# A four-layer sequence kernel: edge tokens in the first query block, more places for background pieces, and the last FFN of two blocks beside the attention

## The chip, the cores and the metric

The kernel runs on one core of one Trainium2 chip. The metric is the device time of one execution in microseconds (us). A NeuronCore has five engines with a queue of instructions each: TensorE (PE; its weight loads are shown apart as PEld), VectorE (DVE), ScalarE (ACT), GpSimd (POOL) and SyncE (SP), which here only issues DMA transfers. An engine works off its own queue in order and waits on semaphores for the others.

## The reference

The input is x of 2048 tokens by 128 features. Four layers follow each other, each adds an attention-like part and a feed-forward part (FFN) to x behind a layer norm (`ln`):

```python
x = x + L0_attn(ln(x))   # 16 heads of width 8
x = x + L0_ffn(ln(x))    # 128 -> 512 -> 128, exact GELU
x = x + L1_attn(ln(x))   # 16 heads of width 64 over all 2048 tokens
x = x + L1_ffn(ln(x))    # silu(x Wg) * (x Wu), 384 hidden, 8-bit weights
x = x + L2_attn(ln(x))   # each token attends to itself and its two neighbours, cyclic in 1024
x = x + L2_ffn(ln(x))    # best one of 8 experts, a 128x128 matrix each
x = x + L3_attn(ln(x))   # a memory: 32 chunks of 64 tokens, one gradient step per chunk
x = x + L3_ffn(ln(x))    # best two of 8 experts and a shared one, 176 hidden each
```

What matters for the order of the work: L1's attention needs all keys and values, but its queries can be taken block by block. Everything behind it works token by token, except for two things. L2's attention needs the first neighbours beyond a block of tokens on either side. L3's memory is serial: step c starts from the state that step c-1 left.

```python
g = grad_fn(W_state, k[:, sl], v[:, sl]) * 0.1        # sl: the chunk's 64 tokens
gn = maximum(norm(g), 1e-6); g = g * minimum(1.0 / gn, 1.0)
(S_state, W_state), Wtraj = scan(step, (S_state, W_state), (g, eta, theta, alpha))
```

## The kernel before

All engine calls are made in one function, `body` (line 71), through a wrapper (`Eng`, line 137), so every row of the profile carries line 147 and the tiles' names tell what it is. The order of the instructions on PE, DVE, ACT and POOL is that of the calls: a planner, run while the program is built, keeps a clock for each engine from cost constants (`note`, line 96) and calls the pieces of many generators in the order that its clocks suggest. The framework places the DMAs on SP.

There are three stretches. The first is layer 0 and the keys and values of layer 1 (0 to 906 us). The second is the **attention stage** (`l1_attn`, line 1066): L1's attention runs over 40 **units**, each one block of queries by one pair of heads. The blocks are the table `QB` in line 33, (first token, tokens, columns): 512, 384, 512, 384 and 256 tokens, with eight pairs each. A unit has 16 **key steps** of 128 keys. A key step is four passes of scores (high part, low parts, and minus the row's maximum) for two heads on PE into two banks, two exponentials P on ACT, then two products with the values on PE. The sums of P over the key steps are taken by POOL (`acg`), and in key steps 14 and 15 by DVE (`acd`). Beside these the maxima of the scores of a later unit are formed (`u_max`, line 425): products km by qh on PE, and a reduction `mx` on DVE that frees the bank. `stage_wo` (line 1023) adds the pairs' share of the output product.

The last stretch is the **tail**: what is left of the layers behind.

Those layers are generators that run in the background of the attention stage: `stage_a` (L1's FFN of 256 tokens), `stage_a2` and `stage_b` (L2's attention), `stage_b2` (its experts), `stage_c` (L3's inputs of 128 tokens), `chunk` (line 1626, one memory step, 32 in all: tiles af, u, ef, dz, rr, gq), `stage_d` (its output), `stage_g` (the router of the last FFN), `stage_e0`, `s_lane` (lines 1872 and 1880, the last FFN: 13 **groups** of up to 128 hidden units per 256 tokens) and `stage_e1` (output). Each `yield` ends a **piece**. A yield says what the next piece needs: a number of PSUM banks (`yield 1`), a time that it should wait (a float), that it has only PE work without a new bank ("T"), or nothing.

`Part.may` (line 202) tells whether a piece may come now: its inputs are due by the planner's clocks, DVE and ACT aren't too far behind, and of the banks that the background uses in the attention stage (the five of `mx`) two stay free. `fill` (line 246) puts pieces into the order until PE's clock has moved by 0.3 us. It is called twice in a key step, behind the maxima and behind the value products (line 1163 on). `fill(lim, "t")` takes only pieces that need neither banks nor PE.

The layers behind need tokens that lie beyond their block: the first tokens of blocks of 256. The **edge tokens** `ex` (1280, 1792 and 2047; line 32) are therefore carried as extra columns by query block 1 (384 tokens, 388 columns), and `stage_m` (line 1314) takes them through L1's FFN to L2's keys and values, into `edge`. `stage_b` of any block waits for `stage_m` ("m" in `s_b`, line 1959), and for `stage_a2` of its neighbour, unless the neighbour's first token is an edge token. `stage_m` can start once query block 1 is through, that is behind unit 15.

In the tail (`tail`, set behind `l1_attn()`) `st`'s three banks join the background's, and five more `s_lane` generators the first two. In the last FFN all groups of a block add into one bank `ac`, which `stage_e0` opens and `stage_e1` adds to x (`xs`) by `add_tok`. In the attention stage `s_e0` lets block b start only when all groups of block b-1 are through.

Of the kernel before, what the change touches and what calls it, by code (L numbers as in the profile page):

```python
# [30 lines left out]
ATANH = (1.0000000039388743, 0.3333315796754013, 0.20012426861749952, 0.13980709417165652, 0.14087328632693624)  # L31
T = dict(lead0=22, more0=4, mgap=0.4, pvq=2, lim0=0.5, fq=(3,), pl=-0.5, pr=1.0, tlow=2, tback=3, late=0.3, pvp="mx", mxp="mx", ex=(1280, 1792, 2047), low=1, lows='ge', keep=1, leave=2, pvn=1, sp=0, rdy=40., eu=2, qg=(22, 16, 10), em=2, el=6, sem=0.2, same=1.2, tsame=3.0, order="hdmBbAaEcCeg", ps=dict(st=3, mx=5), dma=2.3, slack=0.1, lim=0.3, backlog=2.5, lead=(10, 8, 6), pp=7, dve=(14, 15), qp=(1, 1), lanes=2, xl=5,
         QB=[(0, 512, 512), (512, 384, 388), (896, 512, 512), (1408, 384, 384), (1792, 256, 256)])

# [36 lines left out]
def body(ctx: ExitStack, tc: tile.TileContext, x, pa, pb, pc, pi, pd, pr, pr0, pe, pw, out):  # L71
# [122 lines left out]
    class Part:  # L194
# [24 lines left out]
        def step(self):  # L219
            piece[0] = clk["T"]  # L220
            r = next(self.gen, "end")
            self.same = r == "same"
            self.ready = 0.0 if self.same else piece[0] + (r if type(r) is float else 0.0)
            self.pe = r == "T"
            self.banks = r if type(r) is int else 0
            self.seen = len(emitted) if r is False else -1
            if r == "end":
                emitted.add(self.key)
            return r != "end"
# [139 lines left out]
    xnd = dram.tile([128, S], F32, name="xnd")  # L369

    QB = T["QB"]
    EXTRA = T['ex']
    units = [(qb, p) for qb in range(len(QB)) for p in range(NP1)]
    qhh, qfs, kmx, mx1 = {}, {}, {}, {}

    qx = [mid.tile([128, 8], F32R, name=f"qx{i}") for i in range(2)]
    xq = {}

    def u_loadx(qb):
        t0, tn, n = QB[qb]  # L380
        xq[qb] = l1x.tile([128, 512], F32, name="xq", tag="xq", bufs=2)
        if n != tn:
            ge.memset(xq[qb][:, tn:n], 0.0)
            for i, t in enumerate(EXTRA):
                sy.dma_start(xq[qb][:, tn + i:tn + i + 1], xnd[:, t:t + 1])
        sy.dma_start(xq[qb][:, :tn], xnd[:, t0:t0 + tn])

    def u_qprep(u):
        qb, p = units[u]
        if qb not in xq:  # L390
            u_loadx(qb)
        n = QB[qb][2]
        yield 1
        ps = mi()
        mm(ps[:, :n], C("wq", p * 128, 128), xq[qb][:, :n])
        yield
        qf = l1x.tile([128, 512], F32, name="qf", tag="qf")
        se.activation(qf[:, :n], ps[:, :n], AF.Identity, bias=bq8[:, p:p + 1], scale=0.125)
        rel(ps)
        yield  # L400
        qhh[u] = l1q.tile([128, 512], F32R, name="qh", tag="qh")
        se.copy(qhh[u][:, :n], qf[:, :n])
        yield
        qfs[u] = qf
        tn, n = QB[qb][1:]
        if n > tn:
            for e in range(2):
                r = slice(64 * e, 64 * e + 64)
                se.copy(qx[u % 2][r, 4 * e:4 * e + n - tn], qf[r, tn:n])

# [14 lines left out]
    def u_max(u, i):  # L425
# [8 lines left out]
        if 128 * qt == tn:  # L434
            ps = amx()
            mm(ps[0:8], qx[u % 2], kmx[(u, c)])
            ve.tensor_reduce(mx1[u][0:8, 0, 3, c:c + 1], ps[0:8], AX.X, ALU.max)
            rel(ps)
            return 1
# [9 lines left out]
    def u_maxend(u):  # L449
# [6 lines left out]
        if n > tn:  # L456
            ve.tensor_reduce(m[0:8, 0, 3:4], mx[0:8, 0, 3, :], AX.X, ALU.max)
        yield 1
        t = mi()
        if n > tn:  # L460
            te.transpose(t[0:1, 256:264], m[0:8, 0, 3:4], ident[0:8, 0:8])
        for e in range(2):
# [4 lines left out]
        if n > tn:  # L467
            for e in range(2):
                se.mul(mbt[u % 2][64 * e:64 * e + 1, tn:n], t[0:1, 256 + 4 * e:256 + 4 * e + n - tn], -1.0)
        rel(t)  # L470
# [480 lines left out]
    psum_pools(**T["ps"])  # L951
    in0[0] = False
    leave[0] = T["leave"]
# [69 lines left out]
    def stage_wo(qb, part):  # L1023
# [4 lines left out]
        for p in range(2 * part, 2 * part + 2):  # L1028
            mm(ps[:, :n], C("wo", p * 128, 128), O.pop(p)[:, :n], start=(p % 2 == 0), stop=(p % 2 == 1))
            yield  # L1030
        if part == 0:
            w = l1w.tile([128, 512], F32, name="wac", tag="wac", bufs=1)
            se.activation(w[:, :n], ps[:, :n], AF.Identity, bias=bo1)
            rel(ps)
            wacc[qb] = w
            return
# [3 lines left out]
        if part < NP1 // 2 - 1:  # L1040
            return
        del wacc[qb]
        yield 1
        c0, nt = t0 // 128, tn // 128
# [8 lines left out]
        if n != tn:  # L1053
            ne = len(EXTRA)
            xm = edge_x[0] = sm.tile([ne, 128], F32, name="xm", tag="xm", bufs=1)
            for i, t in enumerate(EXTRA):
                sy.dma_start(xm[i:i + 1, :], xs[t % 128:t % 128 + 1, t // 128, :])
            yield 1
# [7 lines left out]
    def l1_attn():  # L1066
        LEAD = dict(zip((256, 384, 512), T["lead"]))
        LEAD.update({260: LEAD[384], 388: LEAD[512]})
        U = len(units)
# [66 lines left out]
        for g in range(16 * U):  # L1136
# [6 lines left out]
            if u + 2 < U:  # L1143
                if k == 1 and units[u + 2][1] == 0:
                    need(("q", u + 1))
                    u_loadx(units[u + 2][0])
                if k == T["qp"][n <= 256] and u + 2 >= EU:
# [13 lines left out]
            for i, (a, b) in enumerate(ops):  # L1161
                for e in range(2):
                    rows = slice(64 * e, 64 * e + 64)
                    mm(pss[e][:, :n], a[rows], b[rows, :n], start=(i == 0), stop=(i == 3), par=e and 0.02)
            for e in range(2):
                pt = pp.tile([128, 512], F32, name="P", tag="P")
# [147 lines left out]
    def stage_m():  # L1314
# [21 lines left out]

        xt = sm.tile([128, 4], F32, name="xtm", tag="xtm", bufs=2)
        yield from norm_T(xt)
        h = sm.tile([128, 12], F32, name="hm", tag="hm", bufs=1)
        for k in range(3):  # L1340
# [3 lines left out]
            yield  # L1344
            th = sm.tile([128, 4], F32, name="thm", tag="thm", bufs=2)
# [3 lines left out]
            ve.scalar_tensor_tensor(h[:, 4 * k:4 * k + ne], th[:, :ne], 0.5, ps[:, 64:64 + ne], ALU.mult, ALU.mult)  # L1349
            rel(ps)  # L1350
            yield 1
        ps = mi()
        for k in range(3):
            mm(ps[:ne, :128], h[:, 4 * k:4 * k + ne], tok(wi, 6 + k), start=(k == 0), stop=(k == 2))
        yield
        ve.tensor_tensor(xm, xm, ps[:ne, :128], ALU.add)
        rel(ps)
        yield
        xt = sm.tile([128, 4], F32, name="xtm", tag="xtm", bufs=2)
        yield from norm_T(xt)  # L1360
        ps = mi()
        for i in range(2):
            mm(ps[:, 4 * i:4 * i + ne], tok(w2m, i), xt[:, :ne])
        yield
        for i in range(2):
            for j, t in enumerate(EXTRA):
                se.activation(edge[:, t // BN, i, int(t % BN > 0):int(t % BN > 0) + 1], ps[:, 4 * i + j:4 * i + j + 1],
                              AF.Identity, bias=b2m[:, i:i + 1])
# [257 lines left out]
    def chunk(b, c):  # L1626
# [48 lines left out]
        ve.scalar_tensor_tensor(u, tht, 2.0, u, ALU.mult, ALU.add)  # L1675
        yield
        mm(da, ef, w2)
# [194 lines left out]
    def stage_e0(b):  # L1872
        d = E[b]
        yield 1
        ac = mi()
        for i in range(BT):
            mm(tok(ac, i), tok(d["rT"][:, 0], i), pes[0:9, 128:256], start=(i == 0), stop=False)
        d["ac"] = ac

    def s_lane(lane):  # L1880

        q = []
        while ("l", NB_ - 1) not in emitted:
# [37 lines left out]
            if d["left"] == 0:  # L1921
                emitted.add(("l", b))
            yield

    def stage_e1(b):
        c0, ac = BT * b, E.pop(b)["ac"]
        add_tok(ac, c0)
        yield
        ov = out.rearrange("(c p) d -> p c d", p=128)
# [188 lines left out]
```

## Time and profile before

| | |
|---|---|
| three timed runs | 2992.95, 3005.0, 3006.38 us (median 3005.0) |
| the profiled execution | 3001.08 us, span 2999.2 us |
| mean granted clock of PE | 0.936 |
| first stretch | 0 to 906 us |
| attention stage | 906 to 2596 us, 1690 us: PE busy 1609.63, DVE 1187.42, ACT 750.20, POOL 1203.47 |
| tail | 2596 to 3000 us, 404 us: PE busy 343.46, DVE 288.45, ACT 159.70, POOL 167.20 |

A row of the profile's groups reads "line engine operation out<-in", the shapes (partitions x elements), the number of instructions, their busy time, the mean of one in ns, and the idle time of the engine just ahead of them with what ended it. A row of the timeline is start, duration, and the same; in brackets stands the wait ahead of it. `mi` is the name of every PSUM bank.

### The profile page before, as it was taken

The numbers are of one execution on the slowest core, as the hardware profiler recorded it, in microseconds if no ns is written. First come the engines' busy times: TensorE is split into PE (matmuls) and PEld (weight loads), VectorE is DVE, ScalarE is ACT, GpSimd is POOL, SyncE is SP. The second block draws the span as 40 slices with busy tenths as digits, with TensorE's granted clock in tenths as the row PEclk, the third lists the DMA queues.
The fourth block names the chain that finished last, engine by engine and source line by source line (L and its number), as shares of the span: only waits on it lengthen the run. The fifth ranks groups of instructions, "written<-read, shape, count | busy, mean of one in ns | idle before, by whom it ended". The sixth has DMA issues, their size and how long they took to land.

```text
span 2999.2 us, 49776 instructions
## 1 busy us (share of the span) xinstructions
PE 2769.9 (92%) x16719; PEld 1307.0 (44%) x16719; DVE 2194.9 (73%) x4699; ACT 1582.9 (53%) x3933; POOL 1522.3 (51%) x1762
## 2 busy tenths in 40 slices
PE   7999999999979899999999999899989898888998
PEld 2222222322234344454444444455544555565666
DVE  7899898898534666566666778887677769787765
ACT  1788887888854444444444444444434334333444
POOL 2400110201127688866776876677767556443444
PEclk9999999999979999999999999999999999776779
DMA  6311231321144333433442332233334343312244
GB/s 142 72 28 22 72 84 17 101 54 46 53 141 135 92 112 110 121 110 111 138 119 87 94 95 87 89 105 108 109 97 114 108 117 94 88 52 61 76 104 115
DMA packets 247749, 275.80 MB, mean 92 GB/s; under 512 B 95747, under 2 KB 183330, under 8 KB 247366
## 3 DMA queue, kind: packets, MB, share of 16 engines
q1 hardware_dynamic: 246630, 272.43, 33.2%
q8 instruction: 132, 2.16, 0.3%
q14 instruction: 123, 1.01, 0.1%
q10 hardware_dynamic: 864, 0.20, 0.0%
HBM read 229.97 MB, written 42.28 MB: 91 GB/s over the span
## 4 chain that ended last, share of the span: by engine, by line
PE 70%; DVE 18%; ACT 6%; issue 3%; DMA 3%; POOL 1%; SPq 0%; ACTq 0%; DVEq 0%; POOLq 0%
PE mi L147 70%; DVE mx L147 5%; ACT P L147 3%; DVE sB L147 1%; DVE o L147 1%; DVE gq L147 1%; DMA ka<-kvd 1%; DVE gt L147 1%; DVE xs L147 1%; ACT kf L147 1%; ACT kh L147 1%; DVE xn L147 1%; DVE sG L147 1%; DVE acd L147 1%; DVE sA L147 0%
## 5 line engine op out<-in xcount | busy, mean ns | idle before, releaser
L147 DVE TENSOR_REDUCE mx<-mi 128x1 f32<-128x512 f32 (+1 forms) x2080 | 1322.1, 683 | 582.8 <-PE mi L147 571.5
L147 ACT ACTIVATE P<-mi 128x512 f32<-128x512 f32 (+3 forms) x2304 | 1137.0, 551 | 1004.1 <-PE mi L147 973.2
L147 POOL TENSOR_TENSOR acg<-acg,P 128x512 f32<-128x512 f32 (+3 forms) x960 | 1011.4, 1083 | 181.8 <-ACT P L147 180.0
L147 PE MATMUL mi<-P,ka 128*64 128x512 f32 (+3 forms) x2560 | 597.6, 546 | 2.3 <-DVE mx L147 2.3
L147 PE MATMUL mi<-qh,ka 64*128 64x512 f32 (+3 forms) x2560 | 521.0, 406 | 9.7 <-DMA ka<-kvd 6.8
L147 PEld LDWEIGHTS mi<-qh,ka 64*128 64x128 f32 x2560 | 247.0, 189 | 382.5 <-issue 347.0
L147 PE MATMUL mi<-kop,qop 48*128 48x512 bf16 x1024 | 348.6, 405 | 24.5 <-DVE mx L147 12.1
L147 PE MATMUL mi<-qop,kop 50*128 50x512 bf16 x1024 | 317.8, 391 | 27.1 <-ACT P L147 24.7
L147 PE MATMUL mi<-P,vop 128*32 128x512 f32 x2048 | 304.3, 623 | 13.9 <-ACT P L147 13.9
L147 POOL TENSOR_SCALAR vep<-mv 128x2 f32<-128x2 f32 (+1 forms) x24 | 5.5, 229 | 495.6 <-DVE mv L147 495.6
L147 PE MATMUL mi<-km,qh 64*128 64x512 f32 x1024 | 225.6, 410 | 30.4 <-DVE mx L147 23.8
L147 PE MATMUL mi<-mbt,onr 64*128 64x512 f32 (+3 forms) x1280 | 228.7, 351 | 1.5 <-DMA mbt<-mb 1.5
L147 PE MATMUL mi<-ql,ka 64*128 64x512 f32 (+3 forms) x1280 | 229.2, 353 | 0.0
L147 PEld LDWEIGHTS mi<-P,ka 128*64 128x64 f32 x2560 | 129.2, 137 | 225.3 <-issue 195.1
L147 PEld LDWEIGHTS <-kop 50*128 50x128 bf16 x1024 | 63.6, 95 | 304.9 <-issue 281.6
L147 POOL TENSOR_TENSOR acg<-P 128x512 f32<-128x512 f32 (+3 forms) x80 | 91.1, 1158 | 202.5 <-DVE acd L147 162.0
L147 PEld LDWEIGHTS mi<-km,qh 64*128 64x128 f32 x1024 | 107.1, 189 | 60.5 <-DVE mx L147 38.5
L147 PEld LDWEIGHTS mi<-mbt,onr 64*128 64x128 f32 x1280 | 124.6, 190 | 13.9 <-DMA mbt<-mb 2.2
L147 PEld LDWEIGHTS mi<-ql,ka 64*128 64x128 f32 x1280 | 125.7, 192 | 0.0
L147 PEld LDWEIGHTS <-qop 48*128 48x128 bf16 x1024 | 72.9, 96 | 97.2 <-issue 82.7
L147 PEld LDWEIGHTS mi<-P,vop 128*32 128x32 f32 x2048 | 55.5, 109 | 119.8 <-issue 90.7
L147 POOL TENSOR_TENSOR kl<-kf,kh 128x512 f32<-128x512 f32 x32 | 40.9, 1278 | 110.9 <-ACT kh L147 82.4
(509 smaller groups left out, 3464.4 us busy)
## 6 DMA issues: line engine op xcount, KB each, us to landing
ka<-kvd SPq DMA_DIRECT2D x320, 384.0 KB
km<-khd SPq DMA_DIRECT2D x159, 256.0 KB
khd<-kh SPq DMA_DIRECT2D x32, 256.0 KB
kvd<-kh SPq DMA_DIRECT2D x32, 256.0 KB
kvd<-kl SPq DMA_DIRECT2D x32, 256.0 KB
kvd<-vt SPq DMA_DIRECT2D x16, 512.0 KB
ka<-in_pw_dram SPq DMA_DIRECT2D x37, 192.0 KB
w3s<-in_pw_dram SPq DMA_DIRECT2D x35, 192.0 KB
```

The source lines that it names most:

```text
L147: r = f(*a, **k)
```

## The change

The diff, cut; what is left out carries a wider edge tile (8 for 4 columns) through `u_maxend` and `stage_m`.

```diff
-T = dict(lead0=22, ..., ex=(1280, 1792, 2047), ...,
-         QB=[(0, 512, 512), (512, 384, 388), (896, 512, 512), (1408, 384, 384), (1792, 256, 256)])
+T = dict(fa=2, ti=(0, 1, 2), tf=1, lead0=22, ..., ex=(256, 768, 1280, 1792, 2047), ...,
+         QB=[(0, 384, 392), (384, 512, 512), (896, 512, 512), (1408, 384, 384), (1792, 256, 256)])
...
-            self.pe = r == "T"
+            self.pe = r == "T" or type(r) is float
...
-    units = [(qb, p) for qb in range(len(QB)) for p in range(NP1)]
+    SEG = [(1, 0, 2), (0, 0, 8), (1, 2, 8), (2, 0, 8), (3, 0, 8), (4, 0, 8)]
+    units = [(qb, p) for qb, p0, p1 in SEG for p in range(p0, p1)]
+    NX = 8
...
-            mm(ps[0:8], qx[u % 2], kmx[(u, c)])
-            ve.tensor_reduce(mx1[u][0:8, 0, 3, c:c + 1], ps[0:8], AX.X, ALU.max)
+            mm(ps[0:2 * NX], qx[u % 2], kmx[(u, c)])
+            ve.tensor_reduce(mx1[u][0:2 * NX, 0, 3, c:c + 1], ps[0:2 * NX], AX.X, ALU.max)
...
-    in0[0] = False
+    in0[0] = True
...
-            yield
+            yield "T" if p % 2 == 0 else 0
-            w = l1w.tile([128, 512], F32, name="wac", tag="wac", bufs=1)
+            w = l1w.tile([128, 512], F32, name="wac", tag="wac", bufs=2)
...
+                if T["tf"] and i in T["ti"]:
+                    fill(9.0, "t")
...
             fill()
+            if T["tf"]:
+                fill(9.0, "t")
...
                     do_pv(*prev.pop(0))
+                    if T["tf"]:
+                        fill(9.0, "t")
                 fill()
+                if T["tf"]:
+                    fill(9.0, "t")
...
-        yield
+        yield "T"
         mm(da, ef, w2)
...
+        own = not tail
-            mm(tok(ac, i), tok(d["rT"][:, 0], i), pes[0:9, 128:256], start=(i == 0), stop=False)
-        d["ac"] = ac
+            mm(tok(ac, i), tok(d["rT"][:, 0], i), pes[0:9, 128:256], start=(i == 0), stop=(own and i == BT - 1))
+        if own:
+            yield
+            add_tok(ac, BT * b)
+        d["ac"] = None if own else ac
...
-            yield T["late"]
+            own = ac is None
+            yield 1 if own else T["late"]
+            if own:
+                ac = mi()
             d["left"] -= 1
+            last = own or d["left"] == 0
             for i in range(BT):
-                mm(tok(ac, i), tok(th[:nr], i), w[:nr, 2, :], start=False, stop=(d["left"] == 0 and i == BT - 1))
+                mm(tok(ac, i), tok(th[:nr], i), w[:nr, 2, :], start=(own and i == 0), stop=(last and i == BT - 1))
+            if own:
+                yield
+                add_tok(ac, BT * b)
...
-            if b and not tail:
-                yield from wait(("l", b - 1))
+            while not tail and b >= T["fa"]:
+                yield False
```

It has three parts.

1. **Edges.** The edge tokens become five (256, 768, 1280, 1792, 2047) and ride with query block 0, now 384 tokens in 392 columns; block 1 is 512. The units run as `SEG` lists them: two pairs of block 1 first, then block 0 whole, then the rest of block 1, then the others. `stage_m` can so start behind unit 9, and `stage_b` needs no neighbour block. The queries' input `xq` is loaded per segment, once more in all; block 1's partial output is held meanwhile in a second `wac` buffer.
2. **Pieces between the passes.** `fill(9.0, "t")` is also called behind the first three score passes, behind each `fill()` and behind the value products. The planner charges 0.12 us where PE's tile shape changes (`in0`), and a piece that waits for a time (float) or a memory step's third product ("T") counts as one that needs PE.
3. **The last FFN beside the attention.** A block whose `stage_e0` comes in the attention stage gives each group a bank of its own, and a sum into `xs` (`add_tok`). Blocks 0 and 1 (`fa` = 2) may do so; the others wait for the tail.

More of the change, by code (lines that the diff above doesn't have):

```diff
@@ L31 @@
 ATANH = (1.0000000039388743, 0.3333315796754013, 0.20012426861749952, 0.13980709417165652, 0.14087328632693624)
-T = dict(lead0=22, more0=4, mgap=0.4, pvq=2, lim0=0.5, fq=(3,), pl=-0.5, pr=1.0, tlow=2, tback=3, late=0.3, pvp="mx", mxp="mx", ex=(1280, 1792, 2047), low=1, lows='ge', keep=1, leave=2, pvn=1, sp=0, rdy=40., eu=2, qg=(22, 16, 10), em=2, el=6, sem=0.2, same=1.2, tsame=3.0, order="hdmBbAaEcCeg", ps=dict(st=3, mx=5), dma=2.3, slack=0.1, lim=0.3, backlog=2.5, lead=(10, 8, 6), pp=7, dve=(14, 15), qp=(1, 1), lanes=2, xl=5,
-         QB=[(0, 512, 512), (512, 384, 388), (896, 512, 512), (1408, 384, 384), (1792, 256, 256)])
+T = dict(fa=2, ti=(0, 1, 2), tf=1, lead0=22, more0=4, mgap=0.4, pvq=2, lim0=0.5, fq=(3,), pl=-0.5, pr=1.0, tlow=2, tback=3, late=0.3, pvp="mx", mxp="mx", ex=(256, 768, 1280, 1792, 2047), low=1, lows='ge', keep=1, leave=2, pvn=1, sp=0, rdy=40., eu=2, qg=(22, 16, 10), em=2, el=6, sem=0.2, same=1.2, tsame=3.0, order="hdmBbAaEcCeg", ps=dict(st=3, mx=5), dma=2.3, slack=0.1, lim=0.3, backlog=2.5, lead=(10, 8, 6), pp=7, dve=(14, 15), qp=(1, 1), lanes=2, xl=5,
+         QB=[(0, 384, 392), (384, 512, 512), (896, 512, 512), (1408, 384, 384), (1792, 256, 256)])
 def _pack_layout(items):
@@ L372, in body, with u_loadx @@
     EXTRA = T['ex']
-    units = [(qb, p) for qb in range(len(QB)) for p in range(NP1)]
+    SEG = [(1, 0, 2), (0, 0, 8), (1, 2, 8), (2, 0, 8), (3, 0, 8), (4, 0, 8)]
+    units = [(qb, p) for qb, p0, p1 in SEG for p in range(p0, p1)]
+    seg = [i for i, (_, p0, p1) in enumerate(SEG) for _ in range(p0, p1)]
+    NX = 8
     qhh, qfs, kmx, mx1 = {}, {}, {}, {}
-    qx = [mid.tile([128, 8], F32R, name=f"qx{i}") for i in range(2)]
+    qx = [mid.tile([128, 2 * NX], F32R, name=f"qx{i}") for i in range(2)]
     xq = {}
-    def u_loadx(qb):
-        t0, tn, n = QB[qb]
-        xq[qb] = l1x.tile([128, 512], F32, name="xq", tag="xq", bufs=2)
+    def u_loadx(i):
+        t0, tn, n = QB[SEG[i][0]]
+        xq[i] = l1x.tile([128, 512], F32, name="xq", tag="xq", bufs=2)
         if n != tn:
[L383 to L386, printed above, removed]
+            ge.memset(xq[i][:, tn:n], 0.0)
+            for j, t in enumerate(EXTRA):
+                sy.dma_start(xq[i][:, tn + j:tn + j + 1], xnd[:, t:t + 1])
+        sy.dma_start(xq[i][:, :tn], xnd[:, t0:t0 + tn])
     def u_qprep(u):
         qb, p = units[u]
-        if qb not in xq:
-            u_loadx(qb)
+        if seg[u] not in xq:
+            u_loadx(seg[u])
         n = QB[qb][2]
@@ L394, in u_qprep @@
         ps = mi()
-        mm(ps[:, :n], C("wq", p * 128, 128), xq[qb][:, :n])
+        mm(ps[:, :n], C("wq", p * 128, 128), xq[seg[u]][:, :n])
         yield
@@ L408, in u_qprep @@
                 r = slice(64 * e, 64 * e + 64)
-                se.copy(qx[u % 2][r, 4 * e:4 * e + n - tn], qf[r, tn:n])
+                se.copy(qx[u % 2][r, NX * e:NX * e + n - tn], qf[r, tn:n])
     def u_qlow(u):
@@ L456, in u_maxend @@
         if n > tn:
-            ve.tensor_reduce(m[0:8, 0, 3:4], mx[0:8, 0, 3, :], AX.X, ALU.max)
+            ve.tensor_reduce(m[0:2 * NX, 0, 3:4], mx[0:2 * NX, 0, 3, :], AX.X, ALU.max)
         yield 1
@@ L460, in u_maxend @@
         if n > tn:
-            te.transpose(t[0:1, 256:264], m[0:8, 0, 3:4], ident[0:8, 0:8])
+            te.transpose(t[0:1, 256:256 + 2 * NX], m[0:2 * NX, 0, 3:4], ident[0:2 * NX, 0:2 * NX])
         for e in range(2):
@@ L468, in u_maxend @@
             for e in range(2):
-                se.mul(mbt[u % 2][64 * e:64 * e + 1, tn:n], t[0:1, 256 + 4 * e:256 + 4 * e + n - tn], -1.0)
+                se.mul(mbt[u % 2][64 * e:64 * e + 1, tn:n], t[0:1, 256 + NX * e:256 + NX * e + n - tn], -1.0)
         rel(t)
@@ L1042, in stage_wo @@
         del wacc[qb]
+        if n != tn:
+            ne = len(EXTRA)
+            xm = edge_x[0] = sm.tile([ne, 128], F32, name="xm", tag="xm", bufs=1)
+            for i, t in enumerate(EXTRA):
+                sy.dma_start(xm[i:i + 1, :], xs[t % 128:t % 128 + 1, t // 128, :])
+            piece[0] = clk["D"]
         yield 1
@@ L1053, in stage_wo @@
         if n != tn:
[L1054 to L1057, printed above, removed]
             yield 1
@@ L1067, in l1_attn @@
         LEAD = dict(zip((256, 384, 512), T["lead"]))
-        LEAD.update({260: LEAD[384], 388: LEAD[512]})
+        LEAD[392] = LEAD[512]
         U = len(units)
@@ L1143, in l1_attn @@
             if u + 2 < U:
-                if k == 1 and units[u + 2][1] == 0:
+                if k == 1 and seg[u + 2] > seg[u + 1]:
                     need(("q", u + 1))
-                    u_loadx(units[u + 2][0])
+                    u_loadx(seg[u + 2])
                 if k == T["qp"][n <= 256] and u + 2 >= EU:
@@ L1335, in norm_T @@
             yield 1
-        xt = sm.tile([128, 4], F32, name="xtm", tag="xtm", bufs=2)
+        xt = sm.tile([128, NX], F32, name="xtm", tag="xtm", bufs=2)
         yield from norm_T(xt)
-        h = sm.tile([128, 12], F32, name="hm", tag="hm", bufs=1)
+        h = sm.tile([128, 3 * NX], F32, name="hm", tag="hm", bufs=1)
         for k in range(3):
@@ L1344, in stage_m @@
             yield
-            th = sm.tile([128, 4], F32, name="thm", tag="thm", bufs=2)
+            th = sm.tile([128, NX], F32, name="thm", tag="thm", bufs=2)
             se.activation(th[:, :ne], ps[:, 0:ne], AF.Tanh, scale=0.5)
@@ L1348, in stage_m @@
             ve.scalar_tensor_tensor(th[:, :ne], th[:, :ne], 1.0, ps[:, 0:ne], ALU.add, ALU.mult)
-            ve.scalar_tensor_tensor(h[:, 4 * k:4 * k + ne], th[:, :ne], 0.5, ps[:, 64:64 + ne], ALU.mult, ALU.mult)
+            ve.scalar_tensor_tensor(h[:, NX * k:NX * k + ne], th[:, :ne], 0.5, ps[:, 64:64 + ne], ALU.mult, ALU.mult)
             rel(ps)
@@ L1353, in stage_m @@
         for k in range(3):
-            mm(ps[:ne, :128], h[:, 4 * k:4 * k + ne], tok(wi, 6 + k), start=(k == 0), stop=(k == 2))
+            mm(ps[:ne, :128], h[:, NX * k:NX * k + ne], tok(wi, 6 + k), start=(k == 0), stop=(k == 2))
         yield
@@ L1358, in stage_m @@
         yield
-        xt = sm.tile([128, 4], F32, name="xtm", tag="xtm", bufs=2)
+        xt = sm.tile([128, NX], F32, name="xtm", tag="xtm", bufs=2)
         yield from norm_T(xt)
@@ L1362, in stage_m @@
         for i in range(2):
-            mm(ps[:, 4 * i:4 * i + ne], tok(w2m, i), xt[:, :ne])
+            mm(ps[:, NX * i:NX * i + ne], tok(w2m, i), xt[:, :ne])
         yield
@@ L1366, in stage_m @@
             for j, t in enumerate(EXTRA):
-                se.activation(edge[:, t // BN, i, int(t % BN > 0):int(t % BN > 0) + 1], ps[:, 4 * i + j:4 * i + j + 1],
+                se.activation(edge[:, t // BN, i, int(t % BN > 0):int(t % BN > 0) + 1], ps[:, NX * i + j:NX * i + j + 1],
                               AF.Identity, bias=b2m[:, i:i + 1])
@@ L1916, in s_lane @@
             ve.scalar_tensor_tensor(th[:nr], th[:nr], 1.0, rb_[:nr], ALU.add, ALU.mult)
-            yield T["late"]
+            own = ac is None
+            yield 1 if own else T["late"]
+            if own:
+                ac = mi()
             d["left"] -= 1
+            last = own or d["left"] == 0
             for i in range(BT):
-                mm(tok(ac, i), tok(th[:nr], i), w[:nr, 2, :], start=False, stop=(d["left"] == 0 and i == BT - 1))
-            if d["left"] == 0:
+                mm(tok(ac, i), tok(th[:nr], i), w[:nr, 2, :], start=(own and i == 0), stop=(last and i == BT - 1))
+            if own:
+                yield
+                add_tok(ac, BT * b)
+                d["done"] = d.get("done", 0) + 1
+                last = d["done"] == NHT3
+            else:
+                last = d["left"] == 0
+            if last:
                 emitted.add(("l", b))
@@ L1926, in stage_e1 @@
         c0, ac = BT * b, E.pop(b)["ac"]
-        add_tok(ac, c0)
-        yield
+        if ac is not None:
+            add_tok(ac, c0)
+            yield
         ov = out.rearrange("(c p) d -> p c d", p=128)
```

## The prediction

> **What bounds the kernel now.** I read the page's totals and slices first, then the stretches of the two stages that the change touches, then single units, and last the waits. The profiled execution took 3001.08 us (span 2999.2), between the three timed runs (2992.95, 3005.0, 3006.38); all sums are against it.
>
> ```profile
> PE 2769.9 (92%) x16719; PEld 1307.0 (44%) x16719; DVE 2194.9 (73%) x4699; ACT 1582.9 (53%) x3933; POOL 1522.3 (51%) x1762
> PE   7999999999979899999999999899989898888998
> PEclk9999999999979999999999999999999999776779
> PE 70%; DVE 18%; ACT 6%; issue 3%; DMA 3%; POOL 1%; SPq 0%; ACTq 0%; DVEq 0%; POOLq 0%
> ```
>
> TensorE (PE) is busy everywhere and is 70% of the chain that ended last, VectorE (DVE) 18%. But the clock row drops to 7 in the slices behind 2550 us: that is the tail, where no attention fills the gaps. By stage (columns: us, then busy PE, PEld, DVE, ACT, POOL, clock, DMA share, GB/s) the attention stage, 906 to 2596 us in two parts, and the tail:
>
> ```profile
> 906.00:1541.00 635.00, 619.83 (x3775) 289.77 (x3776) 387.79 (x646) 301.21 (x645) 486.42 (x454) 0.99 0.39 116
> 1541.00:2596.00 1055.00, 989.80 (x6350) 505.94 (x6347) 799.63 (x1690) 448.99 (x1291) 717.05 (x815) 0.95 0.36 101
> 2596.00:3000.00 404.00, 343.46 (x1715) 256.06 (x1713) 288.45 (x1065) 159.70 (x658) 167.20 (x279) 0.76 0.31 79
> ```
>
> In the attention stage PE is 95% busy at a clock near 1, in the tail 85% at 0.76. So a PE instruction is dearer in the tail than in the attention stage. Moving work forward trades a dear place for a cheap one; the question is whether the cheap place can take it.
>
> **What moves.** I compared the order of instructions on each engine. PE issues 14,895 matmuls in both kernels, but 427 go from the tail (910 to 483) into the attention stage (8225 to 8652). By kind: 26 groups of the last FFN (104 to 78 in the tail), 14 steps of the memory recurrence (18 to 4; the first starts in unit 13 and not in 22), 8 of 10 runs of stage d, 6 of 8 of stage c, 2 of 7 of g. So the change does what it says, and "nothing moves" is no case.
>
> **What the moved work costs in the attention stage.** Prices are start to start of an attention matmul behind the piece, at clock 1. The first half of an FFN group, 1.06 us:
>
> ```profile
> 1597.70 1.13 PE L147 MATMUL mi<-xt,wi 128*128 128x256 f32 x4
> 1598.76 0.50 PE L147 MATMUL mi<-qh,ka 64*128 64x512 f32 x2
> ```
>
> Its second half (two products of 128x128) has no row in this stage; two such (pcs,hb) insert 0.74, so a group is 1.8. A memory step is four small pieces, .58 + .45 + .23 + .46 = 1.72 by the same reading; runs of d 2.5, c 2.6, g 1.7. Sum: 26 x 1.8 + 14 x 1.72 + 8 x 2.5 + 6 x 2.6 + 2 x 1.7 = 46.8 + 24.1 + 20 + 15.6 + 3.4 = **110 us**. The blocks have 2056 columns in all, not 2052; the stage's score and value products are about 1300 us, so +2.5.
>
> The edge rows' larger tiles (16 for 8 rows) are one instruction as before. The extra load of 256 KB of xq and 26 weight loads of 192 KB go onto SP's queue ahead of later ka loads; the DMA share is 0.36 to 0.39 there, and all waits for ka are 20.9 us. I take 0, with as much again, 21, as the upper bound. The change of the planner's price for a tile shape and the new places between passes cost no instruction. The 24 sums that each group with its own bank adds (xs<-xs,mi, 0.44 us a row) are DVE's. Each such group also takes a second bank, of the five that the maxima use, for its product and that sum; a late sum holds the bank, behind which queue the maxima and then PE. That is the same stall as below and is priced there.
>
> **New stalls.** What can late DVE work cost PE? Clean units, in which nothing is inserted, take 40.2 (512 columns) and 34.5 us (384) here:
>
> ```profile
> 1041.50:1081.70 40.20, 40.20 (x236) 17.47 (x234) 24.91 (x41) 20.08 (x37) 33.56 (x26) 1.00 0.37 112
> 1507.00:1541.50 34.50, 33.33 (x236) 17.06 (x234) 23.94 (x42) 16.49 (x38) 26.38 (x26) 1.00 0.44 129
> ```
>
> Summing units by such rows plus the price of what is inserted gives 1586 us for the stage; it took 1690. The 103 us between are stalls, and most have this form:
>
> ```profile
> 2178.15 8.00 DVE L147 SCALAR_TENSOR_TENSOR u<-tht,u 64x32 f32<-64x32 f32 x1
> 2176.28 5.78 POOL L147 TENSOR_TENSOR acg<-acg,P 128x384 f32<-128x384 f32 x6
> 2182.27 3.83 POOL L147 TENSOR_TENSOR acg<-acg,P 128x384 f32<-128x384 f32 x4
> 2187.14 1.39 PE L147 MATMUL mi<-km,qh 64*128 64x512 f32 x2 [6.60 <-DVE mx L147]
> ```
>
> A DVE instruction with its inputs in SBUF, 0.22 us in the tail, lasts 8.00 us across ten of GpSimd's (POOL's) sums; behind it in DVE's queue stand the maxima (mx), whose banks PE needs, and PE waits 6.60 us. Seventeen DVE instructions of the stage last more than 1.5 us over their shortest, together 63 us, 38 of them in memory steps and stage c: 2.7 us for each of the 14 steps. That the mean of the same row differs by stage says so too (xcount, busy, mean ns; the stage, then the tail):
>
> ```profile
> L147 DVE SCALAR_TENSOR_TENSOR u<-tht,u 64x32 f32<-64x32 f32 x14 | 16.0, 1140 | 0.0
> L147 DVE TENSOR_TENSOR gq<-i,dO 32x64 f32<-32x64 f32 x7 | 17.0, 2425 | 0.1
> ```
>
> ```profile
> L147 DVE SCALAR_TENSOR_TENSOR u<-tht,u 64x32 f32<-64x32 f32 x18 | 3.9, 219 | 0.0
> L147 DVE TENSOR_TENSOR gq<-i,dO 32x64 f32<-32x64 f32 x9 | 10.8, 1197 | 0.1
> ```
>
> [...]
>
> For the new stalls I have these ends. Below: the new places between passes let DVE pieces enter up to three times more often in a key step, and in the new order a memory step spans 5 to 6 key steps where it spanned 8 to 12; if that removes the stalls of the 14 old steps as well, -38. Above: if each cluster becomes DVE's. With the stage's own DVE rows I summed what the new order gives each unit: unit 13 has 65 us of DVE against 48 of PE, unit 20 69 against 55, unit 28 58 against 47, unit 36 55 against 39. The heaviest unit before is 22, 47.6 against 44.6, and took 50.2. Eight such dense units times 12 us is +95. The nearest row, 2.7 us a step for 14 more, is +38. I take **+20**: denser memory steps with half the stall each leave the 28 steps at the old sum, and the 26 FFN groups with their 24 DVE sums (some 34 us of DVE) add about half of their time.
>
> So the attention stage is 1690 + 110 + 2.5 + 20 = about 1823.
>
> **What the tail saves.** Its PE instructions are worth 298 us at the stage prices; it took 404, factor 1.356. Left are 298 - 110 = 188, times 1.356 = 255. The middle of the tail is the dearest part:
>
> ```profile
> 2700.00:2800.00 100.00, 86.11 (x386) 62.75 (x385) 69.31 (x264) 37.90 (x177) 40.48 (x69) 0.65 0.27 67
> 2951.00:3000.00 49.00, 40.35 (x205) 32.45 (x204) 24.48 (x51) 21.98 (x56) 22.11 (x28) 0.88 0.45 98
> ```
>
> That part, with 18 memory steps one behind the other (16.3 us apart, 2627 to 2920), shrinks most, which speaks for a few us less; I take 250, a gain of **154**. What is late next is the chain of the last block of tokens, which cannot start before the last output product: in before it ran 16 (wo), 28 (a), 17 (a2), 29 (b), 44 (b2) us to 2730; then c some 30, 4 steps x 16.3 = 65, d and g 31, and the last FFN, 49 before with 23 of 27 half groups behind the last e0, now 17 of 24, so 40. At the old durations this is 300; they were stretched by the work that now leaves, so 300 is the upper end. PE's own 188 at the clock of the last row (0.88) plus its idle 15% is 235 to 250, the lower end.
>
> Sum: 3001 + 110 + 2.5 + 20 - 154 = **2979.5**; I say 2978. The median of the runs shown is 4 us above the profiled execution, so nothing is added for it.
>
> **Rivals.**
> 1. *The places between passes carry DVE's work well.* Old stalls go too (-38 for +20): 1690 + 112 - 38 = 1764, and tail 250: about 2920. For it: memory steps of half the length. Against it: the clusters have more DVE than PE by row sums.
> 2. *The gain is used up.* Stalls grow as before, +38, and the last block's chain keeps the tail at 265 to 300: 3001 + 112 + 38 - 139 = 3012 down to 2997 with a tail of 250; about 3000. For it: 2.7 us a step is the only measured figure.
> 3. *Slower: VectorE becomes the bound in the clusters.* DVE instructions with SBUF inputs lie behind POOL's sums, maxima wait behind them, and PE waits for the maxima's banks. It decides from the point where DVE's row sum of a cluster is above PE's, as it is in units 13, 20, 28 and 36: +95 for +20, so about 3053. For it: those sums. Against it: part of those rows' length is the blocking itself, which a piece entered at a better moment doesn't pay, and maxima may run up to 22 ahead.
>
> **Chances.** Forecast (2960 to 2985) 0.40, rival 1 0.10, rival 2 0.20, rival 3 0.30. A measurement of this kernel can tell about 0.5%, 15 us. Faster is then forecast plus rival 1, 0.50; same 0.20; slower 0.30. Range: rival 1 at 2920 to rival 3 at 3053, 2918 to 3053; the likeliest case alone is 2955 to 2990.
>
> **What would show it.** Right: the last attention unit ends near 1823 - 1690 = 130 us later, the tail is near 250; units that hold memory steps last as long as their clean units plus the inserted PE work; waits for mx stay near their old sum (571.5 us of DVE waiting for mi, PE waiting for mx under 60). Rival 1: the stage ends under 2675, and u and gq rows fall towards 0.2 and 1.2 us. Rival 2: the tail's a to b2 chain keeps 134 us. Rival 3: PE below 90% busy in units 13 to 38, with idle time put down to mx, and DVE near full there. Wrong altogether: if the granted clock in the stage falls below 0.95, which no row of it now suggests, or if ka's loads come late behind the weight loads.

## The result and the profile after

The changed kernel took 3120.08 us (median of 4 runs, 3113.43 to 3125.2) against 3004.75 us for the kernel before: a ratio of 1.0391, 95% interval 1.0358 to 1.0425. It is slower by 115 us; 26 us of gain were forecast, and the time lies outside the range. The page's totals, its slices of PE and of PE's clock, and its chain, after:

```profile
PE 2831.0 (91%) x16719; PEld 1327.6 (43%) x16719; DVE 2301.8 (74%) x4732; ACT 1600.1 (51%) x3930; POOL 1516.3 (49%) x1755
PE   7999999999879999898899989899998888989888
PEclk9999999999889999998889998899998899886878
PE 60%; DVE 22%; ACT 6%; DMA 6%; issue 4%; POOL 1%; SPq 1%; ACTq 0%; POOLq 0%; DVEq 0%
```

PE's share of the chain fell from 70% to 60%, DVE's and the DMAs' rose. The row of the clock, which had its 7s but for one in the tail, now has 8s in many slices of the attention stage. The two stretches (us, then busy PE, PEld, DVE, ACT, POOL, clock, DMA share, GB/s), the attention stage and the tail:

```profile
904.00:2887.00 1983.00, 1827.02 (x10909) 926.11 (x10905) 1426.66 (x2943) 827.59 (x2271) 1256.10 (x1385) 0.91 0.33 96
2887.00:3117.00 230.00, 190.09 (x930) 145.97 (x928) 156.29 (x489) 99.15 (x317) 108.36 (x156) 0.84 0.39 102
```

The tail gave back 174 us (404 to 230). The attention stage took 293 us more (1690 to 1983). To see what it paid for, I split each stretch in three (all in us, from the records of the profile). *Idle* is the sum of the gaps of over 0.15 us between PE's records. *Clock* is half of the time for which the profile's record of the granted clock shows 0.5. *Work* is the rest, my estimate of PE's time at full clock: it takes half clock as half speed, and in the changed kernel four value products of 512 columns (`mi<-P,ka`) in a row take 1.01 us at 1.00 and 1.91 us at 0.50.

| stretch | length | idle | at half clock | clock | work |
|---|---|---|---|---|---|
| attention, before | 1688 | 78 | 116 | 58 | 1551 |
| attention, after | 1983 | 152 | 341 | 171 | 1660 |
| tail, before | 405 | 56 | 195 | 98 | 252 |
| tail, after | 230 | 37 | 73 | 36 | 156 |

The moved work is 109 us in the attention stage (forecast: 112.5). The stage lost 74 us more to idle time and 113 us to the clock. That is 187 us, where I had put 20.

**How one wait becomes both.** The timeline of the changed kernel at 1900 us (start, duration, engine, operation; in brackets the wait ahead), queries for DVE, POOL and PE:

```profile
1900.94 6.78 DVE L147 TENSOR_SCALAR dz<-dzr,rr 64x32 f32<-64x32 f32 x1
```

```profile
1899.79 0.54 POOL L147 TENSOR_TENSOR rr<-rr,mhalf 64x1 f32<-64x1 f32 x1 [3.58 <-DVE rr L147]
1900.31 7.38 POOL L147 TENSOR_TENSOR acg<-acg,P 128x512 f32<-128x512 f32 x6
```

```profile
1904.09 0.33 PE L147 MATMUL mi<-xst,gq 64*64 64x64 f32 x2
1907.78 0.42 PE L147 MATMUL mi<-dz,kcs 64*64 64x32 f32 x2 [3.37 <-DVE dz L147]
1908.34 1.97 PE L147 MATMUL mi<-P,ka 128*64 128x512 f32 x4
```

dz is 64x32 numbers, and its shortest execution here is 0.13 us. It lasts 6.78 us, and ends when POOL's six sums end. POOL had them in a row because it had waited 3.58 us ahead of them for DVE's rr: one step of the memory made both the backlog and the victim. PE's next instruction needs dz and waits 3.37 us. In both traces every change in the record of the clock (87 before, 121 after) lies within 0.01 us of a grid of 3.41 us. Here are four windows on that grid:

```profile
1899.99:1903.41 3.42, 3.42 (x14) 1.07 (x14) 3.42 (x3) 0.85 (x3) 3.42 (x4) 1.00 0.20 80
1903.41:1906.82 3.41, 1.00 (x10) 0.47 (x6) 3.41 (x1) 1.08 (x2) 3.41 (x4) 1.00 0.00 0
1906.82:1910.23 3.41, 2.45 (x8) 0.79 (x8) 3.40 (x7) 0.40 (x2) 0.87 (x1) 0.50 0.02 5
1910.23:1913.65 3.42, 3.42 (x16) 2.78 (x16) 0.55 (x3) 0.81 (x7) 0.00 (x0) 0.50 0.35 115
```

In the second window DVE is 100% "busy" with one small instruction, and PE does 1.00 us of work. With the third the clock is at 0.50. The record of the clock shows it at half from 1906.82 for 23.89 us, seven steps of the grid, though PE works without a gap of over 0.15 us from 1907.78 on until then; a wait of 3.37 us was so followed by 12 us of loss to the clock.

### The profile page after: what moved, and what is told of

It reads as the page before. It is cut to its first block, busy times and chain, and to the rows that moved or that the text cites. A ratio compares the mean times of both kernels' runs of the same rounds, so it can differ in the third digit from the quotient of the medians.

```text
span 3116.3 us, 49722 instructions
## 1 busy us (share of the span) xinstructions
PE 2831.0 (91%) x16719; PEld 1327.6 (43%) x16719; DVE 2301.8 (74%) x4732; ACT 1600.1 (51%) x3930; POOL 1516.3 (49%) x1755
## 4 chain that ended last, share of the span: by engine, by line
PE 60%; DVE 22%; ACT 6%; DMA 6%; issue 4%; POOL 1%; SPq 1%; ACTq 0%; POOLq 0%; DVEq 0%
PE mi L147 60%; DVE mx L147 7%; ACT P L147 3%; DMA rcd<-rc 2%; DMA rb<-rcd 2%; DVE xn L147 1%; DVE gt L147 1%; DVE sB L147 1%; DVE xs L147 1%; DVE gq L147 1%; DVE dz L147 1%; SPq L147 1%; DVE o L147 1%; ACT kf L147 1%; DVE acd L147 1%
## 5 line engine op out<-in xcount | busy, mean ns | idle before, releaser
L147 PE MATMUL mi<-P,ka 128*64 128x512 f32 (+3 forms) x2560 | 629.8, 573 | 0.6 <-ACT qf L147 0.6
L147 PE MATMUL mi<-qh,ka 64*128 64x512 f32 (+3 forms) x2560 | 544.2, 421 | 7.3 <-DMA ka<-kvd 5.5
L147 PEld LDWEIGHTS mi<-qh,ka 64*128 64x128 f32 x2560 | 260.1, 197 | 345.8 <-issue 306.0
L147 PE MATMUL mi<-km,qh 64*128 64x512 f32 x1024 | 236.8, 423 | 43.7 <-DVE mx L147 38.9
L147 PE MATMUL mi<-mbt,onr 64*128 64x512 f32 (+3 forms) x1280 | 239.3, 365 | 1.8 <-DMA mbt<-mb 1.8
L147 PE MATMUL mi<-ql,ka 64*128 64x512 f32 (+3 forms) x1280 | 239.3, 366 | 0.0
L147 PEld LDWEIGHTS mi<-mbt,onr 64*128 64x128 f32 x1280 | 132.7, 200 | 14.7 <-DMA mbt<-mb 2.5
L147 PEld LDWEIGHTS mi<-ql,ka 64*128 64x128 f32 x1280 | 133.1, 202 | 0.0
```

Source lines behind the costliest of these rows:

```text
L147: r = f(*a, **k)
```

## The experiments

Each run stands beside runs of the kernel before on the same chip; ratios are to those, with 95% intervals.

**1. POOL's sums cut to 8 columns, in both kernels.** The kernel so leaves most of the softmax's sums out. The order of instructions stays the same on every engine.

```diff
-eng.tensor_tensor(t[:, :n], t[:, :n], pts[e][:, :n], ALU.add)
+if eng is ge:
+    ge.e.tensor_tensor(t[:, :8], t[:, :8], pts[e][:, :8], ALU.add)
...                                           # the planner is still told n columns; DVE's sums stay
```

> The changed kernel with the same order of instructions on every engine, but POOL's sums of P (acg, behind the first of each unit) go over 8 columns instead of 256 to 512; the sums of the softmax are so left out for the other columns. It frees POOL and takes away what DVE's instructions with SBUF inputs stand behind. Theory A (DVE stands behind POOL's sums, PE's waits and the windows at half clock follow from that): of the 187 us by which the attention stage grew beyond the moved work, at least two thirds go, and the old stalls too; stage below 1800 us, total below 2930 us. Theory B (the pieces of the recurrence come too close behind each other, whatever POOL does): stage above 1900 us, total 3040 to 3110 us.

> The kernel before with the same cut of POOL's sums to 8 columns. It tells what the cut takes from the old order. Theory A: most of the 103 us of stalls go, stage 1600 to 1620 us, total 2900 to 2930 us, and the changed kernel with the cut is no slower than this. Theory B: the cut is worth under 40 us here, total 2965 to 3000 us, and the changed kernel with the cut stays over 60 us slower than this one.

Measured: changed kernel 2883.38 us (0.9619, 0.9563 to 0.9676), kernel before 2905.79 us (0.9694, 0.9636 to 0.9752), with 2 runs each. Theory A holds, and B is out: once POOL's sums are short the change is no slower, and by the medians 22 us faster (not shown beyond noise: the two intervals overlap), close to the forecast 26. The attention stage of the changed kernel with the cut:

```profile
903.00:2654.00 1751.00, 1705.58 (x10903) 872.30 (x10904) 1166.02 (x2943) 822.25 (x2272) 444.51 (x1388) 0.97 0.39 108
```

Its work is 1663 us as in the changed kernel (1660); idle fell from 152 to 42 us and the clock's part from 171 to 46. The old order has some 50 us of the two left with the cut, so of the 187 us by which the change had more of them, some 40 remain. By PE's waits in this stage, DVE ended 140 us of the idle time in the changed kernel, 67 before and 27 with the cut. A rival, that POOL's late sums hold the tiles P and so stop ScalarE and PE, has little room: PE waited 2.1 us for ScalarE's P in the changed kernel, 3.8 us before. What happened to DVE's small instructions (xcount, busy, mean ns), first in the changed kernel, then with the cut:

```profile
L147 DVE TENSOR_SCALAR dz<-dzr,rr 64x32 f32<-64x32 f32 x28 | 35.7, 1276 | 2.8 <-POOL rr L147 2.7
L147 DVE TENSOR_TENSOR gq<-i,dO 32x64 f32<-32x64 f32 x14 | 28.4, 2026 | 0.2
```

```profile
L147 DVE TENSOR_SCALAR dz<-dzr,rr 64x32 f32<-64x32 f32 x28 | 6.7, 238 | 2.8 <-POOL rr L147 2.7
L147 DVE TENSOR_TENSOR gq<-i,dO 32x64 f32<-32x64 f32 x14 | 5.2, 369 | 0.2
```

DVE instructions that last over 1.5 us more than their shortest: 17 in the attention stage before (64 us over), 36 after (129 us), 3 with the cut (7 us).

**2. The parts of the change.** Old blocks and edges with the rest of the change; the change without the calls between passes; the first part alone; the second part alone. The first two edits, cut (the first has the old `QB` too; the last two runs have `fa=0`, and the third the planner's old rules and `tf=0`):

```diff
-SEG = [(1, 0, 2), (0, 0, 8), (1, 2, 8), ...]; ex=(256, 768, 1280, 1792, 2047)   # first run
+SEG = [(0, 0, 8), (1, 0, 8), ...]; ex=(1280, 1792, 2047)
-tf=1                                                                          # second run
+tf=0
```

> The changed kernel with the first part undone: query blocks, their order and the three edge tokens as before; pieces between passes and the last FFN beside the attention stay. In the order of instructions 28 memory steps and 26 FFN groups are in the attention stage, as with the change. If the pieces between the passes carry the loss (theories A and B alike): 3090 to 3150 us. If the new blocks, edges and their loads cost (theory C): 3000 to 3040 us.

> The changed kernel without the second part's extra calls between passes (the two old calls of a key step stay); new blocks, edges, and the last FFN's own banks stay. In the order of instructions the attention stage then holds 18 memory steps and 2 to 3 FFN groups (28 and 26 with the change). If the dense pieces are the loss (A and B): 2980 to 3020 us. If the blocks and edges are (C): 3080 to 3130 us.

> Of the change only the first part: new query blocks, their order, five edge tokens. No extra calls between passes, the planner's rules for shapes and for the two kinds of yield as before, and no last FFN in the attention stage. By the order of instructions 17 memory steps are in the attention stage (14 before) and 841 matmuls in the tail (913 before). If the edges are harmless: 2985 to 3010 us. If they cost by themselves, as the 20 us between the change with and without them suggest: 3010 to 3040 us.

> Of the change only the second part: old blocks and edges, pieces between passes, no last FFN in the attention stage. 28 memory steps are in the attention stage, 606 matmuls in the tail (913 before). If the memory steps carry the loss (their DVE instructions with SBUF inputs stand behind POOL's sums): 3060 to 3100 us. If the last FFN's groups carry it: 2970 to 3010 us.

| parts | median us | ratio (interval) |
|---|---|---|
| passes and FFN, old blocks | 3099.53 | 1.0338 (1.0286 to 1.0390) |
| all but the calls between passes | 3056.64 | 1.0208 (1.0154 to 1.0263) |
| blocks and edges alone | 3034.27 | 1.0099 (1.0066 to 1.0132) |
| passes alone | 3117.08 | 1.0366 (1.0330 to 1.0402) |

The pieces between passes alone cost as much as the whole change. They alone move the memory: 28 of 32 steps are in the attention stage with old blocks too, and 17 with the new blocks alone. So the pieces that they bring, the memory steps above all, are enough for the whole loss. The last FFN isn't needed for it: 3099.53 with it, 3117.08 without (measured beside different runs of the kernel before, and the intervals overlap). The passes alone came out 17 us above their range. The blocks and edges cost 27 us by themselves, for three more memory steps; theory C is right to that extent. There, 26 DVE instructions are long (101 us over), PE stands idle for 124 us of the stage, and 64 us of this are waits for maxima (36 before). So the memory steps aren't the only victims. The run without the calls missed the range of A and B by 37 us. A part of that is the blocks and edges; why the last FFN's own banks or the planner's new rules add more there was not tried.

**3. Can POOL be made to let DVE in?** First a tiny instruction that only writes, behind each sum; then a copy with which POOL waits for DVE's last maximum, ahead of the sums of a key step.

```diff
 eng.tensor_tensor(t[:, :n], t[:, :n], pts[e][:, :n], ALU.add)
+if eng is ge: ge.e.memset(gap, 0.0)                     # first
```

```diff
+if eng is ge and e == 0 and lastmx: ge.e.tensor_copy(gap, lastmx.pop())   # second
 eng.tensor_tensor(t[:, :n], t[:, :n], pts[e][:, :n], ALU.add)
```

> The changed kernel with the same order and all work, plus 960 tiny POOL instructions: behind each sum of P (acg) POOL writes one element of a scrap tile, an instruction that reads nothing from SBUF. In the trace of the change each of the 36 long DVE instructions of the attention stage ends when a run of POOL instructions without a pause ends. If such an instruction between the sums lets DVE in (theory A1), the long ones get no longer than about two sums (2.2 us), the stage's idle time falls from 152 us towards 60, and the total is 2900 to 2990 us. If only a real pause of POOL lets DVE in (A2), nothing is gained: 3100 to 3160 us.

> The kernel before with the same tiny instruction behind each of POOL's sums, order unchanged. A1: a part of the 96 us that the cut sums brought here, 2920 to 2975 us. A2: 2990 to 3020 us.

> The changed kernel, all work kept, order of the other engines unchanged; ahead of the first sum of P of a key step POOL copies one element of the last maximum that DVE has made (mx), so POOL waits there until DVE has come so far (368 such copies). [...] Then no DVE instruction of the attention stage lasts longer than about four sums, the idle time of PE falls from 152 us to under 110, and the total is 2940 to 3060 us. Rival A3: POOL, now late, holds the tiles P, ScalarE and PE wait for those instead: 3110 to 3200 us.

> The kernel before with the same copy that makes POOL wait for DVE's last maximum. A2: 2930 to 2985 us. A3: 3000 to 3080 us.

> Old blocks and edges, pieces between the passes and the last FFN beside the attention, and the copy that makes POOL wait. A2: 2920 to 3040 us, and some 20 us below the changed kernel with the copy. A3: 3090 to 3180 us.

Measured: write-only instruction 3149.28 us (1.0470, 1.0427 to 1.0514), in the kernel before 3058.03 us (1.0176); the copy 3207.3 us (1.0711, 1.0659 to 1.0763), in the kernel before 3083.07 us (1.0293), with old blocks 3167.56 us (1.0572). All five runs were slower than those without the added instruction. In the kernel before, the write-only instruction came out above both its ranges, by 38 us; why it costs that much was not tried. The timeline of the write-only run shows why the first failed:

```profile
1123.84 5.29 DVE L147 TENSOR_TENSOR o<-o,rb 128x392 f32<-128x392 f32 x1 [0.71 <-DMA rb<-rcd]
1124.62 0.09 POOL L1126 MEMSET gap<- 1x1 f32 x1
1124.67 1.02 POOL L147 TENSOR_TENSOR acg<-acg,P 128x392 f32<-128x392 f32 x1
1125.64 0.09 POOL L1126 MEMSET gap<- 1x1 f32 x1
```

DVE's instruction lasts across the small writes (two shown) as it does across sums. So A1 falls. But not every DVE instruction waits for a pause. In the changed kernel this dz came in between two sums that follow each other without one, after 0.66 us:

```profile
1932.62 0.66 DVE L147 TENSOR_SCALAR dz<-dzr,rr 64x32 f32<-64x32 f32 x1
```

```profile
1931.97 2.55 POOL L147 TENSOR_TENSOR acg<-acg,P 128x512 f32<-128x512 f32 x2 [1.73 <-ACT P L147]
```

What decides it was not found. The copy made a real wait, of which the waits of that run show the size:

```profile
POOL gap L1128 <- DVE mx L147: 470.2, 197, 10.7
```

POOL stood 470 us, and then had the sums in a row again: 47 long DVE instructions, 132 us over (36 and 129 without the copy), and 209 us of idle PE. So this wait of POOL did not thin its stream. By the times this is A3: for the changed kernel with the copy A2's range was 2940 to 3060 us. The copy came 7 us above A3's range, and 3 us in the kernel before. By the mechanism it is A3 in part: ScalarE waited 97 us for POOL in that stage (41 without the copy), but DVE itself 149 us (14 without).

**4. Taking DVE's victims away, and due times.** Five operations of the memory leave DVE (dz to ScalarE; the end of u, gq, kcs, hth to POOL); and a longer DMA time in the planner.

```diff
-ve.tensor_scalar(dzn[:, 0, :], dz, rr[:, 3:4], 0.025, ALU.mult, ALU.mult)
+se.mul(dzn[:, 0, :], dz, rr[:, 3:4])       # 0.025 folded into w2; u, gq, kcs, hth: ge for ve
...
-dma=2.3
+dma=6.0
```

> The changed kernel with all work, but five small operations of the memory that read twice from SBUF or are plain scalings leave DVE: dz goes to ScalarE; the last step of u, gq, kcs and hth go to POOL (constants are folded into neighbours). In the trace of the change these five lasted 100 us longer than their shortest (dz 32, gq 25, u 15, hth 15, kcs 13). By the order of instructions the same 28 memory steps and 26 FFN groups are in the attention stage. If DVE standing behind POOL's sums is what costs (theory A), about a third of the stage's 187 us goes: 3040 to 3085 us. If POOL, with more to do, only passes the waiting on (A3): 3105 to 3150 us.

> The changed kernel with the planner's time for a DMA at 6.0 us where it has 2.3. In the trace of the change DVE stands 41.8 us at the head of its queue for the DMA of rb (14.8 before), because o<-o,rb is a piece that the new places between the passes take as soon as the planner thinks it due. 28 memory steps and 24 FFN groups stay in the attention stage. If that standing costs PE (theory D): the wait for rb falls under 15 us and the total to 3050 to 3095 us. If it is hidden: 3105 to 3130 us.

> Old blocks and edges, pieces between the passes, last FFN beside the attention, the five operations off DVE and the longer DMA time in the planner. If theories A and D both hold and add up: 2960 to 3030 us. If neither: 3080 to 3120 us.

> The kernel before with the five operations off DVE and the longer DMA time. Of its 61 us of long DVE instructions 25 to 30 were of these five kinds. Theories A and D: 2950 to 2985 us. Neither: 2990 to 3020 us.

> The kernel before with only the five operations off DVE; with the longer DMA time as well it was 3049 us. If the longer DMA time did that harm: 2970 to 2995 us, since 25 to 30 us of the long DVE instructions go. If the five operations on POOL did it: 3025 to 3055 us.

Measured: operations off DVE 3046.59 us (1.0193, 1.0130 to 1.0256), 74 us under the changed kernel by the medians, 59 by the ratios (1.0391), with the same memory steps in the stage: theory A again, this time with all the work done. In that run, long instructions fell to 27 (92 us over), the clock's part of the stage from 171 to 121 us. Longer DMA time 3100.16 us (1.0342, 1.0302 to 1.0382), between the two ranges: 20 us at most, since the interval overlaps that of the change. This row of the changed kernel's waits, by which DVE stood for rb, is gone with it:

```profile
DVE o L147 <- DMA rb<-rcd: 41.8, 20, 6.4
```

So theory D is a side line. Both with the old blocks: 3035.05 us (1.0130), 5 us above the range for both theories. In the kernel before, both made it slower, 3049.17 us (1.0179), outside both ranges, and the five operations alone faster: 2986.94 us (0.9945, 0.9927 to 0.9962). So there the longer DMA time did the harm; its tail is 436 us, against 385 without it. How, was not tried further.

**5. Fewer sums on POOL.** From the last run with old blocks (3035 us), DVE takes the sums of more key steps.

```diff
-dve=(14, 15)
+dve=(12, 13, 14, 15)        # then (10, 11, 12, 13, 14, 15)
```

> Old blocks, passes, last FFN beside the attention, the five operations off DVE, later DMA due times (this was 3035 us), and now DVE takes the sums of P in key steps 12 to 15 where it took 14 and 15: 160 sums less on POOL (some 170 us), 160 more on DVE (some 80 us at 0.41 to 0.6 us each). If POOL's stream is still what holds DVE: 2960 to 3015 us, and it may pass the kernel before. If DVE has no room left: 3040 to 3090 us.

> As the one with four key steps summed by DVE (2987 us), but six: key steps 10 to 15. Another 160 sums leave POOL; 26 memory steps and 13 FFN groups are then in the attention stage (28 and 21). If POOL's stream is still the larger hindrance: 2945 to 2980 us. If DVE, 75% busy in that stage already, has become the bound: 2990 to 3030 us.

Measured: four key steps 2987.2 us (0.9954, 0.9937 to 0.9972; 8 runs), six 2992.34 us (0.9957, 0.9936 to 0.9979; 10 runs). The attention stage with four:

```profile
903.00:2750.00 1847.00, 1752.35 (x10868) 891.00 (x10868) 1381.43 (x2973) 824.27 (x2287) 1121.12 (x1333) 0.95 0.37 102
```

All 28 memory steps are in this stage, as in the changed kernel, and 21 groups of the last FFN for 26, but POOL has 135 us less to do there, idle is 91 and the clock's part 99 us. This order, with the second and third part of the change in it, passes the kernel before by some 0.5%. But so does the kernel before with the five operations off DVE and none of the change: 2986.94 us, beside the same runs of the kernel before. So these runs show that the loss can be taken away, and not that moving the work then pays. The kernel before with DVE taking more sums was not tried. With six it goes no further, in the range that I gave for DVE as the bound: 20 long instructions are left (60 us over), idle is 82 us, but the planner moved less (work 1638 us), and the tail grew from 239 to 278 us.

## Why the prediction was wrong

**Right:** the exchange of dear for cheap PE time. The moved work was 109 us where 112.5 were summed, group by group. The tail was 230 us where 250 were forecast (its chain did not hold it). With POOL's sums cut the change gained 22 us by the medians, though the intervals overlap.

**Wrong: the step "New stalls", +20 with a bound of +95.** It measured +187. Three things failed in it.

1. *Its unit.* I priced the length of the late DVE instructions, 2.7 us a step, and my example stopped at PE's wait of 6.60 us behind the 8.00 us of u. What the clock does behind such a wait had no term. The granted clock in the trace of before was at half for 10.24 us from 2182.72 on, within that very wait, and I did not look. Over both attention stages, in windows of 3.41 us on the grid on which the clock changes, all 24 full-clock windows with PE busy under 40% were followed by one at half clock, and 14 of 16 with 40 to 50%; of some 840 with over 80%, 1 was. Back to full it went only behind windows that were over 90% busy, 57 times, and 50 times not even then. There were 17 falls to half clock before, 40 after. The prediction named a clock under 0.95 as what would make it "wrong altogether", and said that no row suggested it: the rows to ask were those behind each stall.
2. *Its scale.* I halved the measured 2.7 us of DVE a step, because the places between the passes would help. The halving did not come: dz, gq and u took 36, 28 and 20 us against 12, 17 and 16, at twice the number, so 3.0 us a step where it was 3.2. All long DVE instructions together grew by 65 us, and PE's idle time by 74. And there was a victim that I had not priced. Before, PE waited for maxima; after, it also waits for the moved pieces themselves, since they stand in PE's own queue (us in total, times, longest; before's attention stage, then the changed kernel's):

```profile
PE mi L147 <- DVE mx L147: 36.2, 25, 6.6
PE mi L147 <- DVE dz L147: 1.4, 2, 0.7
```

```profile
PE mi L147 <- DVE mx L147: 51.5, 29, 6.0
PE mi L147 <- DVE dz L147: 24.1, 10, 4.7
PE mi L147 <- DVE e L147: 15.2, 6, 4.4
PE mi L147 <- DVE xn L147: 9.8, 18, 2.0
```

The planner's clocks know nothing of DVE standing behind POOL, so a dense chain is laid out too tight, and a late link can stop PE.
3. *Its bound.* Rival 3 had the mechanism and the sign, but its price came from row sums, as if DVE lacked time. Units 13, 20, 28 and 36 took 76.6, 75.5, 63.0 and 53.3 us; DVE's row sums were 65, 69, 58 and 55, PE's 48, 55, 47 and 39. Even DVE's whole load doesn't explain the first three; in the trace DVE was busy for 61, 59, 52 and 42 us of them, its blocked time included. DVE is 72% busy in this stage, and six of its microseconds in the example are one 0.13 us instruction.

Rival 2's tail (265 to 300 us) was wrong, rival 1 too: old stalls didn't shrink. The largest single term that I left out is the clock: 113 us. Rival 3's 3053 us was nearest, but 67 us short, and DVE was not near full, as its sign asked.

Which DVE instructions come late: the maxima, which read only PSUM, are never among the long ones (1000 in either attention stage, 0.62 to 0.69 us each). All 53 long ones of the two stages (17 before, 36 after) have no PSUM tile among their inputs; 37 are operations on two tensors, 16 copy one or apply scalars to it. And the wait isn't for one POOL instruction alone. Of the 36 long DVE instructions after, each spans 2 to 7 of them, and 32 end where POOL then pauses for 0.4 us or more; three end where it doesn't pause. "Each" in the expectation for the write-only instruction was too much.

## What to carry to other kernels

Price a stall of TensorE with what the clock does behind it (here 113 of the 187 us): look up the granted clock in the windows after each stall that the old trace already has. When work is moved beside a stream of long GpSimd sums (0.73 to 1.30 us each on average here, by their columns), count the moved VectorE instructions that have all their inputs in SBUF, as all 53 long ones here had; each may last until the stream pauses, as 32 of the 36 did, and what stands behind it in VectorE's queue waits too, as the maximum did behind the 8.00 us of u. Thinning the stream and moving the victims to ScalarE and GpSimd are what took the loss away here (3035 to 2987 us, and 3120 to 3047 us). Test them in the old order first: there, moving the victims alone gave the same 2987 us.

## What the runs showed of the hardware

- A VectorE instruction with SBUF inputs can last until GpSimd's stream pauses, and not only until the end of the instruction in progress: 10.9 us across nine GpSimd instructions at the worst (o<-o,rb, before, at 971.8 us). It is no fixed rule: the dz at 1932.62 us came in behind one sum, without a pause.
- A GpSimd instruction of 0.09 us that only writes did not open the stream: 48 long VectorE instructions with 960 of them, 36 without.
- Idle time of TensorE of 1.7 to 2.0 us within one 3.41 us window (busy 40 to 50%) was followed by half clock 14 times in 16. After the change a fall lasted 8.5 us on average (341 us in 40 falls).
